# A four-layer graph-attention kernel: where the second step is prepared, a timetable for some steps, and the place of the copies of G

## The chip, the cores and the metric

The kernel runs on one core of one Trainium2 chip. Every time is device time in microseconds (us) for one execution of the program. Times of a run count from the first to the last instruction; the profile is one execution of the same program, recorded by the hardware profiler, and its times count from the start of its span.

TensorE (PE in the profile) multiplies matrices and writes to PSUM; PEld is its loading of the stationary operand. VectorE is DVE, ScalarE is ACT, GpSimd is POOL. SP is the engine whose queue issues nearly all transfers.

## What is computed

Sixteen samples `x[b]` of 1024 nodes by 256 features pass through four graph-attention layers over one 1024x1024 adjacency. Each layer is

```python
h = jnp.maximum(_layernorm(x), 0.0)
q = h @ W                                  # 256 features: 4 heads of 64, or 1 head of 256
e = leaky_relu(e_src[:, :, None] + e_dst[:, None, :])
attn = softmax(where(adj > 0, e, -inf))    # over the neighbours
x = x + elu(attn @ q)                      # relu in the last layer
```

Layers 0 and 2 have four heads, layers 1 and 3 have one. All arithmetic is float32.

## The kernel before

The work is cut into 64 **steps**, one for each pair of sample and layer. Four samples are in flight at a time (four streams), and `order_of_steps` writes the order of the 64 steps out: steps 0, 1 and 2 are layer 0 of samples 0, 1 and 2; step 3 is layer 1 of sample 0; then four-head and one-head steps alternate for most of the run. A stream comes back after three to five steps.

A step has three parts.

**Preparation** (`preparation(n)`) is a list of 21 pieces: statistics of the two halves of x on DVE (`stats`, L222), their combination on POOL (`combine_all`, L245 to L257), normalisation of the two halves on ACT (`normalise`, L263), and for each half two transposes (L271 on PE, L272 on ACT) and four projections (L282 on PE, L284 on ACT, followed by L290 and L292 on ACT and L294 on POOL). At the end `factors` (L300, L301) and `rows` (L306, L308) put a vector G for each head into a tile `gT`, and a transfer on the SP queue (L310) writes it to DRAM. `fetch_heads` then issues transfers (L324) that bring each head's G back, spread over all partitions, as `gs`.

**Aggregation**: for each head ACT copies `gs` into PSUM as `g` (`broadcast`, L330), DVE makes eight tiles `w` of 128x1024 from it (`weights`, L335), and PE multiplies them with the projected features (`aggregate`, L351). ACT takes the sums out of PSUM as `y` (L366). Each step has eight **groups** of aggregation: of a four-head step a group is half of the rows of one head, of a one-head step an eighth of the rows. There are two PSUM buffers for `g`, two for the sums, and 18 buffers for `w`, so DVE can be ahead of PE by 18 tiles.

**The end of a step** (`finish`): division, ELU and the addition to x, on DVE (L383, L392, L405), POOL (L393, L406) and ACT (L399).

The engines each work through their instructions in the order in which the program emits them, and this order is written by hand. The main loop goes through the groups; after each it emits pieces of the end of the step before, then those preparation pieces of later steps that are due, and then up to six (one-head: three) tiles `w`:

```python
emit_tiles(place[n, h, C - 1] + 1, must=True)
aggregate(n, h, i0, per)
...
prepare(8 * n + k)
ahead = 6 if per > 1 else 3
emit_tiles(min(done["tiles"] + ahead, done["free"] + WBUFS))
```

When a piece is due is said by an **agenda** of 21 numbers, in groups. For step n they are added to `8 * (n - 2)`, two steps ahead. `FOUR` serves four-head steps, `ONE` one-head steps, `SOON` the first ones, `FIRST` step 1 (its numbers are absolute). Where the stream isn't free at the first number of `FOUR`, `LATE` is taken instead, with a later start: before the change this falls on steps 7, 9 and 60, whose streams rested three steps in between (most four-head steps have rested four). A copy of G is emitted inside `emit_tiles`, when the tile four places ahead of the next tile belongs to a new head, and thus after the pieces of its group.

In the opening, before the main loop, step 0 is prepared at once, mixed with the building of the adjacency masks (`sign`, L178, L192, L195, L199). The transfers of x for samples 2 and 3 (`load`) and of the weights of layers 2 and 3 are issued at the end of the opening.

Of the kernel before, what the change touches and what calls it, by code (L numbers as in the profile page):

```python
# [38 lines left out]
WBUFS = 18  # L39
# [2 lines left out]

FOUR = (-8, -8, -5, -3, -2, -1, -1, 0, 0, 0, 0, 0, 0, 2, 2, 2, 2, 3, 8, 8, 10)
ONE = (2, 2, 2, 4, 4, 5, 5, 6, 6, 6, 6, 6, 6, 8, 8, 8, 8, 8, 10, 10, 12)
SOON = (0, 0, 0, 1, 2, 3, 3, 4, 4, 5, 5, 5, 5, 6, 6, 7, 7, 8, 9, 9, 11)
FIRST = (-2, -2, -2, -1, -1, 0, 0, 0, 0, 1, 1, 1, 1, 2, 2, 2, 2, 3, 3, 3, 5)
LATE = (0, 0, 0, 1, 1, 2, 2, 3, 3, 3, 3, 3, 3, 4, 4, 4, 4, 5, 6, 6, 8)


LAYERS = [
    (4, 0.2, 0, 0),
    (1, 0.2, 0, 0),
    (4, 0.2, 128, 1),
    (1, 0.01, 0, 1),
]
# [3 lines left out]
def kernel(ctx: ExitStack, tc: tile.TileContext, x, adj, ws, avs, out):  # L61
    nc = tc.nc
    B, N, F = x.shape
    C = N // P
# [46 lines left out]
    def load_weights(l, queue=nc.sync):  # L111
        H = LAYERS[l][0]
        for k in range(K):
            queue.dma_start(out=heads_of(wx[l], H)[:, k, :, 0:F // H],
                            in_=ws[l][k * P:(k + 1) * P, :].rearrange("p (h d) -> p h d", h=H))
# [87 lines left out]
    def load(b, parts=1):  # L203
        xs[b] = xpool.tile([P, C, F], F32, name="x")
        xb = x[b].rearrange("(p c) f -> p c f", p=P)
        for i in range(parts):
            q = slice(i * C // parts, (i + 1) * C // parts)
            nc.sync.dma_start(out=xs[b][:, q], in_=xb[:, q])
# [112 lines left out]
    def fetch(n, h):  # L321

        gs = state[n]["gs", h] = work.tile([P, N], F32, name="gs", bufs=2)
        nc.sync.dma_start(out=gs, in_=state[n]["grow"][h].rearrange("c i -> (c i)")  # L324
                          .partition_broadcast(P))

    def broadcast(n, h):

        g = state[n]["g", h] = ps_g.tile([P, N], F32, name="g")
        nc.scalar.activation(g, state[n]["gs", h], AF.Copy)  # L330

    def weights(n, h, jc):

        w = state[n]["w", h, jc] = work.tile([P, N], F32, name="w", bufs=WBUFS)
        nc.vector.scalar_tensor_tensor(w, state[n]["g", h], state[n]["rcol"][:, jc, h:h + 1],  # L335
                                       masks[LAYERS[steps[n][1]][3]][:, jc, :],
                                       op0=ALU.max, op1=ALU.mult)
# [88 lines left out]
    def groups(n):  # L426
        if LAYERS[steps[n][1]][0] == 1:
            return [(0, i, 1) for i in range(C)]
        return [(h, i, HALF) for h in range(LAYERS[steps[n][1]][0]) for i in (0, HALF)]

    tiles = [(n, h, jc) for n, (b, l) in enumerate(steps) for h in range(LAYERS[l][0])
             for jc in range(C)]
    place = {t: i for i, t in enumerate(tiles)}
    done = {"tiles": 0, "g": 0, "gs": 0, "rows": 0, "free": 0, "prepared": 0}
    agenda = []

    def prepare(upto):

        while agenda and agenda[0][0] <= upto:
            _, n, piece, last = agenda.pop(0)  # L440
            piece()
            if last:
                done["prepared"] = n + 1

    def plan(n):
        new = preparation(n)
        agenda.extend((at, n, piece, i == len(new) - 1) for i, (at, piece) in enumerate(new))
        agenda.sort(key=lambda a: a[:2])

    def fetch_heads(below=0):  # L450

        done["rows"] = max(done["rows"], below)
        while done["gs"] < min(done["g"] + 2 * C, len(tiles)):
            n, h, _ = tiles[done["gs"]]
            if n >= done["rows"]:
                break
            fetch(n, h)
            done["gs"] += C

    def emit_tiles(upto, must=False):  # L460
        while done["tiles"] < min(upto, len(tiles)):
            i = done["tiles"]

            while done["g"] <= min(i + C // 2, len(tiles) - 1):
                n, h, _ = tiles[done["g"]]
                if n >= done["prepared"]:
                    if i < done["g"] or not must:
                        break
                    prepare(max(a[0] for a in agenda if a[1] == n))
                broadcast(n, h)  # L470
                done["g"] += C
                fetch_heads()
            if i >= done["g"]:
                return
            weights(*tiles[i])
            done["tiles"] += 1

    last, agenda_of = {}, []
    for n, (b, l) in enumerate(steps):

        free = 8 * (last[b % STREAMS] + 1) + (8 if l == 0 else 2) if b % STREAMS in last else -99
        last[b % STREAMS] = n
        start = 8 * (n - 2)
        kind = ONE if LAYERS[l][0] == 1 else SOON if n < 4 else FOUR
        if free > start + kind[0]:
            kind = LATE
            start = max(free, agenda_of[-1][0] + 5, start - LATE[7])
        agenda_of.append([start + k for k in kind] if n > 1 else FIRST)
        if n > 2:

            assert agenda_of[n][7] >= 8 * (n - 2)
            was = agenda_of[n - 1]
            assert agenda_of[n][3] >= was[5] and agenda_of[n][4] >= was[11]
    ending = []
    later = {}
    with tc.manual_schedule():
        blocks = [mask_rows(c) for c in range(C)]
        layer = [weight_columns(l) for l in range(L)]
        layer[0][0](nc.scalar)
        load(0, 2)  # L500
        load_weights(0)
        for c in range(C):
            blocks[c][0]()
        load(1)
        load_weights(1)
        nc.scalar.activation(warm, half1, AF.Exp)
        nc.vector.tensor_copy(identb, ident)
        layer[0][1]()
        first = [piece for _, piece in preparation(0)]

        def sign(c):

            if c < C:
                blocks[c][1]()
                blocks[c][2]()
            if c > 0:
                blocks[c - 1][3]()

        for i in (0, 1, 3, 4):
            first[i]()  # L520
        layer[0][2]()
        first[5]()
        first[6]()
        layer[0][3]()
        sign(0)
        for i, c in ((7, 1), (9, 2), (11, 3), (13, 4), (15, 5)):
            first[i]()
            first[i + 1]()
            sign(c)
        for piece in first[17:]:  # L530
            piece()
        for c in (4, 5, 0, 1, 2, 3):
            blocks[c][4]()
        sign(6)
        sign(7)
        sign(8)
        done["prepared"] = 1
        plan(1)
        planned = 2
        for _ in range(2):  # L540
            agenda.pop(0)[2]()
        emit_tiles(C, must=True)
        blocks[6][4]()
        blocks[7][4]()
        prepare(-1)
        for i in range(2, STREAMS):
            load_weights(i)
            load(i)

        for l, at in ((1, 1), (2, 8 * 3 + 3), (3, 8 * 5 + 3)):  # L550
            for i, piece in zip((0, 1, 2, 8), layer[l]):
                later[at + i] = piece
        for n in range(len(steps)):
            for k, (h, i0, per) in enumerate(groups(n)):
                while planned < len(steps) and min(
                        a[0] for a in agenda_of[planned:planned + 2]) <= 8 * n + k:
                    plan(planned)
                    planned += 1
                emit_tiles(place[n, h, C - 1] + 1, must=True)
                aggregate(n, h, i0, per)  # L560
                if i0 + per == C:
                    done["free"] = place[n, h, C - 1] + 1
                while ending and ending[0][0] <= k:
                    ending.pop(0)[1]()
                if 8 * n + k in later:
                    later[8 * n + k]()
                prepare(8 * n + k)
                ahead = 6 if per > 1 else 3
                emit_tiles(min(done["tiles"] + ahead, done["free"] + WBUFS))
            for _, piece in ending:  # L570
                piece()
            ending = finish(n) if n < len(steps) - 1 else []
# [35 lines left out]
```

## Time and profile before

| | |
|---|---|
| time of three runs | 2640.95 to 2642.32 us, median 2642.26 |
| span of the profile | 2639.2 us |
| PE busy | 2539.8 us (96%) |
| DVE busy | 2041.7 us (77%) |
| ACT busy | 1133.4 us (43%) |
| POOL busy | 1021.5 us (39%) |
| mean granted clock of TensorE | 0.989 |

PE is the busiest engine by far. Its busy time leaves 99 us of the span, and a part of its work is also done at a lower clock. The profile's table of 40 slices of 66 us shows that most slices leave PE about 1 us idle; the first few, the seventh and the last four leave more.

### The profile page before, as it was taken

The page shows a single profiled execution, that of the slowest core. Times are in us where ns is not written, and L with a number is a line of the kernel's source. Part 1 is how long each engine was busy: PE and PEld are TensorE (multiplying, and loading weights), DVE is VectorE, ACT ScalarE, POOL GpSimd, SP SyncE. Part 2 cuts the span into 40 slices and gives each one's busy share as a digit, 9 for nine tenths or more (in the row PEclk, how much of TensorE's full clock was granted, in tenths as well). Part 3 has the DMA queues.
Part 4 walks back from the last instruction along what each step waited for, and adds up shares of the span by engine and source line. Part 5 has one row for each costly group of instructions (what it writes and reads, how often), then busy time and mean ns, then how long its engine had stood idle before and what let it go on. Part 6 is the DMA issues. An engine that isn't in the chain of part 4 may idle for free.

```text
span 2639.2 us, 87794 instructions
## 1 busy us (share of the span) xinstructions
PE 2539.8 (96%) x40088; PEld 2256.5 (86%) x40088; DVE 2041.7 (77%) x2144; ACT 1133.4 (43%) x2502; POOL 1021.5 (39%) x1040
## 2 busy tenths in 40 slices
PE   6899998999999999999999999999999999999899
PEld 4788887888888888888898888888888888888888
DVE  7888566877778877778877778877778877777973
ACT  4343443344444344544344444344444344443341
POOL 2234353423433434443323444433433334444231
PEclk8999999999999999999999999999999999999999
DMA  4101001111112100102211101101112200111101
GB/s 176 51 27 42 26 26 34 42 49 67 50 58 74 42 19 34 42 34 74 74 54 62 42 34 42 42 20 65 50 58 74 74 19 34 42 34 43 51 18 56
DMA packets 36987, 128.98 MB, mean 49 GB/s; under 512 B 6278, under 2 KB 9094, under 8 KB 34696
## 3 DMA queue, kind: packets, MB, share of 16 engines
q1 hardware_dynamic: 36606, 123.36, 13.3%
q8 instruction: 314, 5.14, 0.8%
q14 instruction: 57, 0.47, 0.1%
q10 hardware_dynamic: 10, 0.00, 0.0%
HBM read 105.91 MB, written 17.43 MB: 47 GB/s over the span
## 4 chain that ended last, share of the span: by engine, by line
PE 66%; DVE 17%; POOL 7%; ACT 6%; issue 3%; DMA 0%; DVEq 0%; ACTq 0%
PE acc L351 46%; PE pp L282 15%; DVE w L335 10%; PE pp L271 4%; POOL x L406 3%; DVE e L405 3%; DVE bn L222 2%; ACT xn L263 2%; POOL rstd L251 2%; ACT e L399 1%; DVE e L392 1%; ACT whx L284 1%; ACT rcol L290 0%; ACT gcol L301 0%; ACT whx L292 0%
## 5 line engine op out<-in xcount | busy, mean ns | idle before, releaser
L351 PE MATMUL acc<-whx,w 128*64 128x65 f32 x36864 | 1911.6, 241 | 26.0 <-DVE w L335 20.9
L351 PEld LDWEIGHTS acc<-whx,w 128*64 128x64 f32 x36864 | 1747.2, 145 | 171.6 <-issue 31.2
L335 DVE SCALAR_TENSOR_TENSOR w<-g,rcol,mask 128x1024 f32<-128x1024 f32 x1280 | 1540.6, 1273 | 445.5 <-PE acc L351 387.4
L366 ACT ACTIVATE y<-acc 128x260 f32<-128x260 f32 (+1 forms) x504 | 194.4, 386 | 1097.5 <-PE acc L351 1097.5
L294 POOL TENSOR_TENSOR whx<-whx 128x1024 f32<-128x1024 f32 x128 | 256.4, 2003 | 667.1 <-ACT whx L292 667.1
L282 PE MATMUL pp<-wx,hT 128*128 128x264 f32 (+1 forms) x2048 | 488.6, 390 | 18.8 <-ACT whx L284 11.2
L393 POOL TENSOR_TENSOR y<-y,r 128x1024 f32<-128x1024 f32 x126 | 264.3, 2108 | 618.7 <-DVE e L392 490.8
L282 PEld LDWEIGHTS pp<-wx,hT 128*128 128x128 f32 x2048 | 379.6, 191 | 98.7 <-ACT whx L284 23.5
L406 POOL TENSOR_TENSOR x<-x,e 128x1024 f32<-128x1024 f32 x96 | 238.1, 2486 | 161.0 <-DVE e L405 155.5
L263 ACT ACTIVATE xn<-x,shift,rstd 128x256 f32<-128x256 f32 x512 | 261.3, 590 | 87.9 <-POOL shift L257 85.8
L284 ACT ACTIVATE whx<-pp 128x264 f32<-128x264 f32 (+1 forms) x512 | 195.7, 386 | 236.4 <-PE pp L282 236.1
L222 DVE BATCH_NORM_STATS2 bn<-x 128x6 f32<-128x256 f32 x512 | 175.8, 410 | 58.0 <-POOL x L406 54.6
L405 DVE SCALAR_TENSOR_TENSOR e<-e,y 128x1024 f32<-128x1024 f32 x96 | 175.6, 1839 | 41.7 <-ACT e L399 35.5
L271 PE MATMUL pp<-ident,xn 128*128 128x128 f32 x1024 | 168.6, 284 | 32.1 <-ACT xn L263 28.4
L271 PEld LDWEIGHTS pp<-ident,xn 128*128 128x128 f32 x1024 | 119.3, 141 | 83.2 <-ACT xn L263 53.6
L330 ACT ACTIVATE g<-gs 128x1024 f32<-128x1024 f32 x160 | 163.6, 1024 | 8.1 <-DVE w L335 4.1
L272 ACT ACTIVATE hT<-pp 128x512 f32<-128x512 f32 x256 | 136.8, 585 | 1.9 <-PE pp L271 0.5
L251 POOL TENSOR_TENSOR rstd<-rstd,neghalf 128x8 f32<-128x8 f32 (+1 forms) x65 | 107.0, 1647 | 12.6 <-DVE shift L252 7.6
L399 ACT ACTIVATE e<-e 128x1024 f32<-128x1024 f32 x96 | 100.7, 1049 | 23.9 <-DVE e L392 20.0
L392 DVE SCALAR_TENSOR_TENSOR e<-y,r 128x1024 f32<-128x1024 f32 x64 | 75.5, 1221 | 2.2
L408 DVE SCALAR_TENSOR_TENSOR x<-y,x 128x1024 f32<-128x1024 f32 x30 | 43.3, 1444 | 10.0 <-POOL y L393 10.0
L245 POOL TENSOR_TENSOR dev<-bn 128x8 f32<-128x8 f32 x63 | 13.2, 209 | 89.8 <-DVE bn L222 89.8
(63 smaller groups left out, 401.7 us busy)
## 6 DMA issues: line engine op xcount, KB each, us to landing
gs<-grow SPq DMA_DIRECT2D x160, 512.0 KB
x<-in_x SPq DMA_DIRECT2D x15, 1024.0 KB
out<-x SPq DMA_DIRECT2D x30, 512.0 KB
w<-in_adj SPq DMA_DIRECT2D x8, 512.0 KB
x<-in_x SPq DMA_DIRECT2D x2, 512.0 KB
wx<-in_L_gnn_W SPq DMA_DIRECT2D x8, 128.0 KB
out<-x SPq DMA_DIRECT2D x8, 128.0 KB
grow<-gT SPq DMA_DIRECT2D x32, 16.0 KB
```

The source lines that it names most:

```text
L222: nc.vector.bn_stats(bn[:, c, :], xs[b][:, c, :])
L263: nc.scalar.activation(xn[:, q, :], xs[b][:, c, :], AF.Identity, bias=st["shift"][:, c:c + 1], scale=st["rstd"][:, c:c + 1])
L271: nc.tensor.transpose(pt[:, q, :], st["xn", half][:, q, k * P:(k + 1) * P], ident)
L282: nc.tensor.matmul(pw, lhsT=st["hT", half][:, k, q * P:(q + 1) * P], rhs=wx[l][:, k, :], start=(k == 0), stop=(k == K - 1))
L284: nc.scalar.activation(st["whx"][:, c, :], pw, AF.Copy)
L294: nc.gpsimd.tensor_tensor(wh[:, :, :, 0:D], wh[:, :, :, 0:D], wh[:, :, :, D:D + 1].to_broadcast([P, HALF, H, D]), op=ALU.mult)
L335: nc.vector.scalar_tensor_tensor(w, state[n]["g", h], state[n]["rcol"][:, jc, h:h + 1], masks[LAYERS[steps[n][1]][3]][:, jc, :], op0=ALU.m ...
L351: nc.tensor.matmul(acc[o % P:o % P + cols, q, :], lhsT=st["w", h, jc][:, o:o + cols], rhs=st["whx"][:, jc, h * (D + 1):(h + 1) * (D + 1)], ...
L366: nc.scalar.activation(st["y"][:, i0:i0 + per, h, :], acc, AF.Copy)
L393: nc.gpsimd.tensor_tensor(yh, yh, rb, op=ALU.mult)
L405: nc.vector.scalar_tensor_tensor(e, e, -1.0, yh, op0=ALU.add, op1=ALU.max)
L406: nc.gpsimd.tensor_add(xh, xh, e)
```

## The change

The change has four parts, all of them in the order of emission; no instruction is new and none is left out.

1. **Opening.** Step 1's statistics and their combination are emitted before the last three mask blocks, its normalisation right after the first eight tiles `w`, and everything else of its preparation, up to `rows`, before the main loop begins, so that PE has step 1's transposes and projections before step 0's first aggregation. They used to be spread over the groups of step 0. The new `FIRST` says this: nearly all its numbers are -1.
2. **Agendas.** A new agenda `SHORT`, `FOUR` with its first four pieces later (from -4 on, not from -8), is taken by four-head steps whose stream isn't free for `FOUR` in time: steps 7, 9 and 60. `LATE` isn't reached by them any more. Step 4 takes `SOON` and not `FOUR`.
3. **Copies of G.** A function `emit_heads` emits the copies that fall due in a group ahead of that group's preparation pieces, as far as the tiles of the head before last have all been emitted.
4. `emit_tiles` calls it too, and forces a step's preparation only where the next tile needs it.

```diff
+SHORT = (-4, -4, -4, -2, -2, -1, -1, 0, 0, 0, 0, 0, 0, 2, 2, 2, 2, 3, 8, 8, 10)
-FIRST = (-2, -2, -2, -1, -1, 0, 0, 0, 0, 1, 1, 1, 1, 2, 2, 2, 2, 3, 3, 3, 5)
+FIRST = (-2, -2, -2, -1, -1, -1, -1, -1, -1, -1, -1, -1, -1, -1, -1, -1, -1, -1, -1, -1, 3)
...
+    def emit_heads(i):
+        while done["g"] <= min(i + C // 2, done["tiles"] + C, len(tiles) - 1):
+            n, h, _ = tiles[done["g"]]
+            if n >= done["prepared"]:
+                break
+            broadcast(n, h)
+            done["g"] += C
+            fetch_heads()
+
     def emit_tiles(upto, must=False):
         while done["tiles"] < min(upto, len(tiles)):
             i = done["tiles"]
-            while done["g"] <= min(i + C // 2, len(tiles) - 1):
-                n, h, _ = tiles[done["g"]]
-                if n >= done["prepared"]:
-                    if i < done["g"] or not must:
-                        break
-                    prepare(max(a[0] for a in agenda if a[1] == n))
-                broadcast(n, h)
-                done["g"] += C
-                fetch_heads()
+            if i == done["g"] and tiles[i][0] >= done["prepared"] and must:
+                prepare(max(a[0] for a in agenda if a[1] == tiles[i][0]))
+            emit_heads(i)
...
-        kind = ONE if LAYERS[l][0] == 1 else SOON if n < 4 else FOUR
+        kind = ONE if LAYERS[l][0] == 1 else SOON if n < 5 else FOUR
+        if kind is FOUR and free > start + kind[0]:
+            kind = SHORT
         if free > start + kind[0]:
             kind = LATE
...
+        done["prepared"] = 1
+        plan(1)
+        planned = 2
+        prepare(-2)
         sign(6)
         sign(7)
         sign(8)
-        done["prepared"] = 1
-        plan(1)
-        planned = 2
+        emit_tiles(C, must=True)
         for _ in range(2):
             agenda.pop(0)[2]()
-        emit_tiles(C, must=True)
         blocks[6][4]()
         blocks[7][4]()
         prepare(-1)
         for i in range(2, STREAMS):
             load_weights(i)
             load(i)
...
+                upto = min(done["tiles"] + (6 if per > 1 else 3), done["free"] + WBUFS)
+                emit_heads(upto - 1)
                 if 8 * n + k in later:
                     later[8 * n + k]()
                 prepare(8 * n + k)
-                ahead = 6 if per > 1 else 3
-                emit_tiles(min(done["tiles"] + ahead, done["free"] + WBUFS))
+                emit_tiles(upto)
```

## The prediction, made before the changed kernel was run

> **What bounds the kernel now.** I read the page's slices first, then PE's waits by stretch, then the timelines of the stretches with waits.
>
> ```profile
> PE   6899998999999999999999999999999999999899
> PEclk8999999999999999999999999999999999999999
> ```
>
> Each digit is 66 us. From the ninth slice to the thirty-sixth PE has about 1 us idle a slice, in waits of 0.2 to 0.5 us; DVE waits there for PE (344.9 us in total between 470 and 2380 us, for buffers of w). So the middle is bound by PE's work, and a change of order gains next to nothing there. What can be won lies in the opening, in slices five to seven, and in the end. The opening on DVE and PE:
>
> ```profile
> 41.31 9.61 DVE L335 SCALAR_TENSOR_TENSOR w<-g,rcol,mask 128x1024 f32<-128x1024 f32 x8
> 50.84 2.70 DVE L222 BATCH_NORM_STATS2 bn<-x 128x6 f32<-128x256 f32 x8
> 53.46 19.14 DVE L335 SCALAR_TENSOR_TENSOR w<-g,rcol,mask 128x1024 f32<-128x1024 f32 x16
> 78.80 2.47 DVE L335 SCALAR_TENSOR_TENSOR w<-g,rcol,mask 128x1024 f32<-128x1024 f32 x2 [6.20 <-ACT g L330]
> ...
> 95.77 19.16 DVE L335 SCALAR_TENSOR_TENSOR w<-g,rcol,mask 128x1024 f32<-128x1024 f32 x16 [4.01 <-ACT g L330]
> ...
> 179.98 1.23 DVE L405 SCALAR_TENSOR_TENSOR e<-e,y 128x1024 f32<-128x1024 f32 x1 [9.35 <-ACT e L399]
> ```
>
> ```profile
> 42.73 0.48 PE L351 MATMUL acc<-whx,w 128*64 128x65 f32 x4 [5.21 <-DVE w L335]
> ...
> 185.92 22.57 PE L351 MATMUL acc<-whx,w 128*64 128x65 f32 x656
> 208.32 0.27 PE L306 MATMUL pp<-ident,gcol 128*32 128x128 f32 x1
> 208.43 1.90 PE L351 MATMUL acc<-whx,w 128*128 128x257 f32 x8
> ```
>
> PE has little to do from 31 to 51 us; then it is busy until DVE becomes the limit, from 96 to 165 us (DVE busy 68.93 of 69.00 us there, PE 58.70). DVE loses 6.20 and 4.01 us waiting for copies of G that stand behind preparation pieces on ACT. Step 3 starts on PE at 208.43. The transfers of the opening on SP's queue:
>
> ```profile
> 41.40 1.24 SPq L114 DMA_DIRECT2D wx<-in_L_gnn_W  x2
> 42.69 0.62 SPq L208 DMA_DIRECT2D x<-in_x  x1
> ```
>
> This is x of sample 2, which the statistics at 50.84 read without a wait. The later losses, on PE:
>
> ```profile
> 331.27 0.70 PE L351 MATMUL acc<-whx,w 128*128 128x257 f32 x2 [0.49 <-DVE w L335]
> ...
> 352.87 0.33 PE L271 MATMUL pp<-ident,xn 128*128 128x128 f32 x1 [1.89 <-ACT xn L263]
> ```
>
> ```profile
> 425.10 10.69 PE L351 MATMUL acc<-whx,w 128*128 128x257 f32 x48 [1.02 <-ACT y L366]
> 444.18 2.81 PE L271 MATMUL pp<-ident,xn 128*128 128x128 f32 x8 [8.38 <-ACT xn L263]
> 446.77 5.42 PE L351 MATMUL acc<-whx,w 128*128 128x257 f32 x16
> ```
>
> ```profile
> 414.85 7.24 DVE L335 SCALAR_TENSOR_TENSOR w<-g,rcol,mask 128x1024 f32<-128x1024 f32 x6 [1.38 <-ACT g L330]
> 422.01 0.34 DVE L383 RECIPROCAL r<-y 128x32 f32<-128x32 f32 x1
> ```
>
> ```profile
> 2406.30 0.33 PE L271 MATMUL pp<-ident,xn 128*128 128x128 f32 x1 [1.50 <-ACT xn L263]
> ```
>
> In each PE waits for a normalised x whose chain (end of the stream's last step, statistics, combination, normalisation) is late.
>
> **What the Trainium skill says.** "PSUM — Partial Sum Buffer", § Engine vs sequencer instructions, says that the queues of ScalarE, VectorE and GpSimd are strictly first in, first out; the trace agrees (the copy at 77.76 stood behind evacuations and normalisations on ACT while DVE waited 6.20 us). "TensorE: Matmul & The Clock Gate", Part 1, says that an idle PE falls to half its clock and comes back after a busy window of some 3.4 us. The trace agrees: granted clock 0.50 from 41 to 51 us, and after the 8.38 us wait eight transposes take 2.81 us instead of 1.10 to 1.30. "DMA: Bandwidth & Descriptors", on issuing engines not being separate queues, says that all transfers share the same 16 engines; what matters below is only the order on the issuing queue.
>
> **Part 1, the opening.** It moves 16 transposes (2.4 us) and 8 projections (3.83 us for four: 7.7), 10.1 us in all, from between the groups of step 0 into PE's gap. DVE's statistics of step 1 (2.70) go into its 3.34 us wait at 31 us, so the first tile comes when the copy of G is there, about 39.9 rather than 41.31.
> Then ACT: copies done at 40.9, normalisation 4.04, two masks 1.92, evacuation of two transposes 1.09: 48.0. PE: four projections 3.83, second half's transposes with evacuation 2.27 (92.54 to 94.81 in the old rows), four projections 3.83: 57.9; evacuation, exponentials, factors and rows some 2.5: 60.4. PE starts cold; half clock until 51 to 54.4 adds 1.5 to 3.1. So gT of step 1 is ready at about 62.5, and step 0's first group runs from there and not from 50.98.
> By itself this is about even: PE is later by 11.5 at the end of the first group and has 10.4 less to do. But the write of gT (L310) now stands on SP's queue **ahead** of the weights of layer 2 and of x of sample 2, and it waits for gT. So x of sample 2 is issued at 62.5 + 0.8 + 1.2 = 64.5, not at 42.69. Landing: at least 4.3 after issue (half of x was issued at 0.72 and awaited till 5.05), at most 8.2 (42.69 to 50.84); I take 6: 70.5. Behind it on DVE stand the statistics of step 2, emitted before tiles 8 to 13, and behind these all tiles: DVE, done with tile 7 at 49.4, idles for about 21 us. That is more than the 6.20 + 4.01 + 9.35 us of waits that the parts remove (the last two since copies and ends no longer stand behind so many pieces).
> From 70.5 DVE runs without a gap, since w buffers come free in time: statistics 2.7, then tiles 8 to 87, 80 x 1.195 (19.14/16) = 95.6, and between them columns of layer 1 3.3, two ends of steps 2 x (2.7 + 2.4), statistics of steps 3 and 4 2 x 2.7: 187.7. PE waits at that tile; then 3/4 of the group 2.9, three groups at 3.88, eight projections 7.7, transposes 1.2: step 3 starts at 211.1 instead of 208.43. Loss 2.7; with x two earlier or later and up to 3 for cold clock and copies that wait for DVE, -1 to +6. I take **3 slower**.
>
> **Part 2, agendas.** Step 9's `SHORT` takes its six tiles (7.24) and their copies out of DVE's way at 414 to 422: `rows` of step 9 falls in 8.0.0 and the tiles start in 8.0.2 (step, head, group), as in every later pair. So the division of step 7 comes at 413.9 instead of 422.01, and 3.65 us of tiles leave the path before its last addition: 11 us earlier in a chain that was 8.38 late. Wait 8.38 + 1.02, cold transposes 1.6, cold group 5.42 - 3.48 = 1.9: 12.9, of which the later pairs keep 0.8 (two 0.17 waits and slow transposes at 525.80). Gain **12**.
> Step 7's does the same at 331 to 355: the division of step 5, at 335.90, can come at about 331. The waits of 0.98, 1.89 and 0.48 and the cold group (5.19 - 3.48) go: 5.0, taken as **4.5**.
> Step 60: its statistics move one group (3.7 us) ahead, more than the 1.50 + 0.48 us of wait; with slow transposes **2.4**, of which the later end, where DVE is the limit, takes nothing (its first tile at 2430 follows PE).
> Step 4's move to `SOON` is in the sum of part 1.
>
> **Part 3, copies.** In the pairs of the middle the order on ACT changes once: the third head's copy stands before the evacuation of two transposes (1.02 us later). Behind these PE has a whole group (3.9) before it reads them, which hides it. ACT might wait in the copy for DVE; the old copies waited 4.1 us for DVE in all of the run, and in the middle the tile in question is done 10 us before (about 530 against 540.9). Zero.
>
> **Sum:** +3 - 12 - 4.5 - 2.4 = -15.9: 2642.3 - 15.9 = 2626.4.
>
> **Rivals.** (a) The opening gains: if x of sample 2 came at about 50 as before, PE (from 62.5: 24 groups 93, preparation of steps 2 to 4 30.3, small ones 3, and some 11 of waits for DVE) reaches step 3 at about 200: 8 gained, 2642.3 - 8 - 18.9 = 2615. Against it stands the queue's order; for it, the gap of 20 us on PE. (b) The idle DVE costs more, as the copies wait for DVE with evacuations behind them and PE is cold: opening 10 slower, 2633. (c) The 8.38 us wait only moves, since POOL's additions (5.57) and combination (4.2) remain: gain 4 of 12 with the rest as forecast, 2634; with (b) 2640, hardly a change. (d) Slower: the copies hold up ACT in the middle, 1 us for each of some 27 pairs on PE's path, +27 - 16: 2653. Against it: the 3.9 us of slack.
>
> **How the numbers follow.** Forecast (2620 to 2632) 0.57, (a) 0.12, (b) 0.13, (c) 0.12, (d) 0.06. Faster by over 0.2% (below 2637): forecast, (a), (b) and a third of (c), 0.86; within it 0.08, from (c) with (b); slower 0.06. The range leaves out the lower part of (a), the end of (c) and (d): 2616 to 2636.
>
> **What would show it.** Right: a DVE wait of about 20 us for the DMA of x before L222 at some 70 us; no DVE wait for g of 4 us or more before 200; step 3's first group (128x257) near 211; no wait over 1 us for xn between 340 and 460 nor at 2406; waits of the middle as before. Wrong: no such DVE gap (then (a)), a wait for xn still at about 440 (c), or ACT waiting tens of us for DVE in L330 copies (d).

## The result and the profile after

The changed kernel takes 2628.74 us in the median of four runs (2627.74 to 2632.07); the kernel before took 2641.61 us in four runs beside them (2639.95 to 2642.32). The ratio is 0.9954 with a 95% interval of 0.9937 to 0.9972: faster by some 12 to 13 us. The span of the profile falls from 2639.2 to 2626.9 us, by 12.3.

The sum of the forecast, 2626.4, is 2.3 us off, but its two main terms are off in opposite directions and partly make up for each other. The opening costs 8.4 us, not 3; the agendas bring 20.7 us, not 18.9. The opening can be separated from the rest, because PE has done exactly the same instructions in all kernels of this study when it comes to the four small matmuls that bound the scores of layer 3 (L154 before, L156 after), in step 6. I use this row as a checkpoint. It is the timeline of PE, of before and then of after; the columns are start, length, engine, line, operation, output and inputs, tile, elements and count.

```profile
343.42 0.50 PE L154 MATMUL pp<-sq,ones 128*128 128x1 f32 x4
```

```profile
351.80 0.50 PE L156 MATMUL pp<-sq,ones 128*128 128x1 f32 x4
```

After is 8.4 us later here. From here to the end of the span it needs 2626.9 - 351.8 = 2275.1 us, where before needed 2639.2 - 343.4 = 2295.8: 20.7 us less.

The slices of after, as they were shown for before:

```profile
PE   6889999999999999999999999999999999999899
PEclk8889999999999999999999999999999999999999
```

The second and third slice (66 to 198 us) have lost a tenth of the clock, and the third also one of PE. The seventh (396 to 462 us) shows no dip any more, where before had an 8. The loss lies in the opening, the gain where `SHORT` is taken; the experiments below try both. Now the rows behind them. The queue of SP in the opening, in after:

```profile
61.51 0.69 SPq L312 DMA_DIRECT2D grow<-gT  x1
62.25 2.14 SPq L116 DMA_DIRECT2D wx<-in_L_gnn_W  x2
64.43 0.61 SPq L210 DMA_DIRECT2D x<-in_x  x1
```

Before issued this x (sample 2) at 42.69. Now the write of `gT` stands ahead of it, and that write had to wait for the whole preparation of step 1. DVE in after, with the wait ahead of a row and its releaser in brackets:

```profile
40.16 9.63 DVE L337 SCALAR_TENSOR_TENSOR w<-g,rcol,mask 128x1024 f32<-128x1024 f32 x8 [0.95 <-ACT g L332]
69.43 2.71 DVE L224 BATCH_NORM_STATS2 bn<-x 128x6 f32<-128x256 f32 x8 [19.64 <-DMA x<-in_x]
72.05 21.53 DVE L337 SCALAR_TENSOR_TENSOR w<-g,rcol,mask 128x1024 f32<-128x1024 f32 x18
...
182.88 1.23 DVE L407 SCALAR_TENSOR_TENSOR e<-e,y 128x1024 f32<-128x1024 f32 x1 [4.02 <-ACT e L401]
```

The statistics of step 2 wait 19.64 us for that x, and 18 tiles stand behind them that needed nothing from it. The two waits for copies of G (6.20 and 4.01 in before) are gone, and the wait for the exponential has shrunk from 9.35 to 4.02. PE in after:

```profile
47.66 5.93 PE L284 MATMUL pp<-wx,hT 128*128 128x264 f32 x16 [2.93 <-ACT hT L274]
...
61.11 7.69 PE L353 MATMUL acc<-whx,w 128*64 128x65 f32 x256
73.47 0.49 PE L353 MATMUL acc<-whx,w 128*64 128x65 f32 x4 [4.68 <-DVE w L337]
...
173.01 3.81 PE L284 MATMUL pp<-wx,hT 128*128 128x258 f32 x8 [4.44 <-ACT whx L286]
...
214.98 7.11 PE L353 MATMUL acc<-whx,w 128*128 128x257 f32 x32
```

PE uses its old gap for the preparation of step 1 (from 42 to 61 us), runs two groups with the eight tiles that DVE had made before its wait and then, from 73, works at the pace of DVE's single tiles. Three stretches of after show it; the columns are the stretch, its length, the busy time of PE, PEld, DVE, ACT and POOL with the number of instructions, the granted clock, and the share and rate of DMA.

```profile
61.00:69.00 8.00, 7.79 (x257) 7.55 (x256) 0.00 (x0) 1.74 (x4) 1.25 (x1) 1.00 0.55 172
73.00:82.00 9.00, 3.68 (x34) 2.38 (x35) 9.00 (x9) 2.08 (x4) 2.92 (x7) 0.50 0.06 24
82.00:166.00 84.00, 79.12 (x1965) 73.25 (x1965) 83.80 (x84) 32.44 (x66) 20.68 (x21) 0.93 0.13 47
```

DVE does nothing at all from 61 to 69 us while PE is busy; then DVE is busy 9.00 of 9.00 us while PE, at half clock, works 3.68; and up to 166 DVE stays full (83.80 of 84.00). What DVE lost before 69 us can't be made up in that time.

The later places are those of the forecast. PE in after, where before waited 8.38 us at 444.18:

```profile
437.33 0.66 PE L273 MATMUL pp<-ident,xn 128*128 128x128 f32 x2
438.15 0.33 PE L273 MATMUL pp<-ident,xn 128*128 128x128 f32 x1 [0.16 <-ACT xn L265]
438.64 0.76 PE L273 MATMUL pp<-ident,xn 128*128 128x128 f32 x5 [0.16 <-ACT xn L265]
439.24 3.64 PE L353 MATMUL acc<-whx,w 128*128 128x257 f32 x16
```

PE where before waited 1.89 us at 352.87, and where it waited 1.50 us at 2406.30:

```profile
359.20 1.03 PE L273 MATMUL pp<-ident,xn 128*128 128x128 f32 x8
360.07 3.64 PE L353 MATMUL acc<-whx,w 128*128 128x257 f32 x16
...
2394.80 1.41 PE L273 MATMUL pp<-ident,xn 128*128 128x128 f32 x8
2396.05 3.64 PE L353 MATMUL acc<-whx,w 128*128 128x257 f32 x16
```

In all three places the wait is gone (two of 0.16 us are left in the first), and the group behind the transposes takes 3.64 us; after the long wait it took 5.42.

### The profile page after: what moved, and what is told of

It is laid out like the page before. It is cut to its first block, busy times and chain, and to the rows that moved or that the text cites. A ratio compares the mean times of both kernels' runs of the same rounds, so it can differ in the third digit from the quotient of the medians.

```text
span 2626.9 us, 87790 instructions
## 1 busy us (share of the span) xinstructions
PE 2536.5 (97%) x40088; PEld 2254.3 (86%) x40088; DVE 2046.0 (78%) x2144; ACT 1128.9 (43%) x2502; POOL 1020.9 (39%) x1040
## 4 chain that ended last, share of the span: by engine, by line
PE 64%; DVE 18%; POOL 7%; ACT 6%; issue 4%; DMA 1%; SPq 0%; DVEq 0%; ACTq 0%
PE acc L353 44%; PE pp L284 15%; DVE w L337 11%; PE pp L273 4%; POOL x L408 4%; DVE e L407 3%; DVE bn L224 2%; ACT xn L265 2%; POOL rstd L253 2%; ACT e L401 1%; DVE e L394 1%; ACT whx L286 1%; ACT rcol L292 0%; DMA x<-in_x 0%; ACT whx L294 0%
## 5 line engine op out<-in xcount | busy, mean ns | idle before, releaser
L353 PE MATMUL acc<-whx,w 128*64 128x65 f32 x36864 | 1905.3, 241 | 23.0 <-DVE w L337 20.7
```

Source lines behind the costliest of these rows:

```text
L353: nc.tensor.matmul(acc[o % P:o % P + cols, q, :], lhsT=st["w", h, jc][:, o:o + cols], rhs=st["whx"][:, jc, h * (D + 1):(h + 1) * (D + 1)], ...
```

## The experiments

Two questions were open after the result. First, why does the opening cost what it costs: because x of sample 2 stands behind the write of `gT` on one queue, or because the new opening itself is worse (a cold PE, and copies and evacuations in each other's way)? Second, do the agendas bring the later gain alone? All kernels were timed beside the kernel before, and the ratios are to it. Four experiments (x first, the opening of before, the opening alone, the agendas alone) shared runs of before with a median of 2642.45 us, the other four shared runs with a median of 2643.32; beside the changed kernel it was 2641.61. So a difference between kernels of different sets is certain only to some 2 us.

**The load of x ahead of the write.** The loads at the end of the opening (x of samples 2 and 3, and weights) are issued ahead of the rest of step 1's preparation; nothing else is changed in the changed kernel.

```diff
-        prepare(-1)
         for i in range(2, STREAMS):
             load_weights(i)
             load(i)
+        prepare(-1)
```

> The changed kernel with one edit: the transfers of the weights of layers 2 and 3 and of x of samples 2 and 3 are issued before step 1's rows and not behind them. Theory Q (queue): the opening costs about 10 us (step 3's first group at 214.98 instead of 204.74) because x of sample 2 stands on SP's queue behind the write of step 1's gT. Then DVE's wait of 19.64 us for the transfer of x goes, DVE waits later and shorter for w buffers, and step 3 starts at 200 to 205: 2628.7 - 12 = 2617 (2613 to 2620). Rival F (front-loading): it costs because PE makes all of step 1's preparation, partly at half clock, before its first aggregation. Then DVE's wait turns into one for w buffers and step 3 still starts near 215: 2627 to 2630.

2615.38 us (2615.06 to 2615.83), ratio 0.9895 (0.988 to 0.991); 13.4 us less than the changed kernel, whose interval doesn't touch this one. DVE in this kernel:

```profile
49.99 2.71 DVE L224 BATCH_NORM_STATS2 bn<-x 128x6 f32<-128x256 f32 x8 [0.32 <-DMA x<-in_x]
52.62 9.61 DVE L337 SCALAR_TENSOR_TENSOR w<-g,rcol,mask 128x1024 f32<-128x1024 f32 x8
66.41 12.01 DVE L337 SCALAR_TENSOR_TENSOR w<-g,rcol,mask 128x1024 f32<-128x1024 f32 x10 [4.18 <-ACT g L332]
```

The wait for x is 0.32 us instead of 19.64. PE still reaches the first aggregation only at 61.07, but now finds tiles for three groups in a row. The second row is where step 3 starts:

```profile
61.07 11.42 PE L353 MATMUL acc<-whx,w 128*64 128x65 f32 x384
...
199.01 7.11 PE L353 MATMUL acc<-whx,w 128*128 128x257 f32 x32
```

Step 3 starts at 199.01, 16 us before the changed kernel's 214.98 and 5.7 before the old kernel's. The queue's order is the cause of the loss; the new opening as such gains.

**The late x left late, tiles in front of the statistics.** If the queue only hurts because of what stands behind the statistics on DVE, then it is enough to put tiles ahead of them. Step 2 gets an agenda of its own; x of sample 2 is issued as late as in the changed kernel.

```diff
+        if n == 2:
+            kind = (2, 2, 2, 2, 2) + SOON[5:]
```

> The changed kernel (x of sample 2 still behind the write of step 1's gT) with one edit: step 2's statistics and normalisation stand two groups later, behind tiles 8 to 19. Theory: the late x costs only because DVE's statistics wait for it in front of these tiles; then DVE makes tiles 8 to 17 while x is on its way, its wait for x is under 5 us and step 3 starts at 200 to 204: 2628.7 - 12 = 2617. Rival: the late x costs by itself, since step 2's preparation comes late for PE: 2624 or more.

2616.51 us (2615.05 to 2617.5), ratio 0.9898 (0.9883 to 0.9914). DVE in this kernel:

```profile
39.82 19.16 DVE L337 SCALAR_TENSOR_TENSOR w<-g,rcol,mask 128x1024 f32<-128x1024 f32 x16 [1.28 <-ACT g L332]
65.58 4.86 DVE L337 SCALAR_TENSOR_TENSOR w<-g,rcol,mask 128x1024 f32<-128x1024 f32 x4 [6.60 <-ACT g L332]
70.35 2.70 DVE L224 BATCH_NORM_STATS2 bn<-x 128x6 f32<-128x256 f32 x8
```

Twenty tiles are done before the statistics at 70.35, which then find x there. Nearly the whole of the loss is gone with the transfer as late as ever (issued at 63.85). So the transfer's time was no loss in itself: the in-order queue of DVE turned it into one.

The 6.60 us are a wait for the copy of step 0's third G. That G doesn't depend on step 1's `gT`; the copy stands on ACT behind the evacuation of the first group, which waits for PE:

```profile
64.23 0.39 ACT L368 ACTIVATE y<-acc 128x260 f32<-128x260 f32 x1 [3.63 <-PE acc L353]
64.52 1.02 ACT L332 ACTIVATE g<-gs 128x1024 f32<-128x1024 f32 x1
```

PE starts that group late because it makes step 1's preparation first. This is a cost of the new opening itself; the first experiment has it too, with 4.18 us.

**The changed kernel with the opening of before.** `FIRST` and the order of the opening go back; agendas and copies stay.

```diff
-FIRST = (-2, -2, -2, -1, -1, -1, -1, -1, -1, -1, -1, -1, -1, -1, -1, -1, -1, -1, -1, -1, 3)
+FIRST = (-2, -2, -2, -1, -1, 0, 0, 0, 0, 1, 1, 1, 1, 2, 2, 2, 2, 3, 3, 3, 5)
...
-        prepare(-2)
         sign(6)
         sign(7)
         sign(8)
...
-        emit_tiles(C, must=True)
         for _ in range(2):
             agenda.pop(0)[2]()
+        emit_tiles(C, must=True)
```

> The changed kernel with the opening and the agenda of step 1 as before (parts 2 and 3 alone). If parts 2 and 3 bring what the two traces say between step 3 and the end (22.5 us) and are without effect on the opening: 2641.6 - 22.5 = 2619. If the copies ahead of the pieces also take away the 6.20 and 4.01 us for which DVE waited for g, and DVE is the limit behind them, up to 8 less: 2611. If those gains needed the new opening: above 2625.

2623.43 us (2620.95 to 2627.14), ratio 0.9926 (0.9911 to 0.9941). It passes the checkpoint at 343.72, where the kernel before is at 343.42. So the changed kernel would be some 5.3 us faster without its first part: no run of either kernel reaches into the range of the other, though the intervals of the two ratios just touch. In the profiles this is 8.1 us at the checkpoint, of which 2.7 are lost again in the rest; no single row was found for these.

**The new opening alone, on the kernel before.** The same edit the other way round.

> The kernel before with the new opening and the new agenda of step 1 only (part 1 alone). Theory: the part by itself costs what step 3's start shows, 10 us: 2641.6 + 10 = 2652, and more, up to 2656, since copies of G still stand behind pieces on ACT. Rival: the cost comes from the parts together (copies that wait for DVE ahead of evacuations); then this is within 4 us of 2642.

2652.48 us (2650.19 to 2654.66), ratio 1.0037 (1.0023 to 1.0051): 10 us slower than before, and measurably so. The wait for x is there (20.05 us), the checkpoint comes at 351.59, 8.2 us late. The waits of the old agendas stay; PE in this kernel:

```profile
361.05 0.33 PE L271 MATMUL pp<-ident,xn 128*128 128x128 f32 x1 [1.90 <-ACT xn L263]
...
451.93 2.80 PE L271 MATMUL pp<-ident,xn 128*128 128x128 f32 x8 [8.41 <-ACT xn L263]
```

Both are as long as in before (1.89 and 8.38), though PE comes to them 8 us later. So these waits don't depend on how late the kernel runs; the chain behind them moves along with it.

**The agendas alone, on the kernel before.**

```diff
+SHORT = (-4, -4, -4, -2, -2, -1, -1, 0, 0, 0, 0, 0, 0, 2, 2, 2, 2, 3, 8, 8, 10)
...
-        kind = ONE if LAYERS[l][0] == 1 else SOON if n < 4 else FOUR
+        kind = ONE if LAYERS[l][0] == 1 else SOON if n < 5 else FOUR
+        if kind is FOUR and free > start + kind[0]:
+            kind = SHORT
```

> The kernel before with SHORT for steps 7, 9 and 60 and SOON for step 4, copies and opening as before (part 2 alone). Theory: the waits for xn at 352, 444 and 2406 go by the agendas alone, so 2641.6 - 5 - 12.5 - 2.4 = 2622 (2619 to 2625). Rival: the copies ahead of the pieces are needed for the second; then the wait near 444 keeps 4 us or more, and the time is 2628 or more.

2622.31 us (2620.83 to 2624.64), ratio 0.9922 (0.9907 to 0.9936): 20.1 us less than before, more than the whole change. The wait for `xn` near 440 is two waits of 0.16, while the waits for copies of G in the opening (6.67 and 4.01) stay. The gain lies behind the checkpoint, in the places of `SHORT`, and it comes without the other parts.

**The copies alone, on the kernel before**, that is `emit_heads` and its calls.

> The kernel before with the copies of G ahead of a group's pieces and nothing else (part 3 alone). Theory from the runs so far (agendas alone -20.1 us, agendas and copies -19.0): the copies bring nothing by themselves, 2642 within 4 us. Rival: they take the 6.20 and 4.01 us for which DVE waited for g out of the opening, and PE gains most of it: 2634 or less.

2645.26 us in 20 runs (2641.47 to 2649.32), ratio 1.001 (1.0003 to 1.0017): slower by 0.1%, nearly nothing. The first of the two waits for copies of G goes, but the second grows; DVE in this kernel:

```profile
96.34 14.39 DVE L337 SCALAR_TENSOR_TENSOR w<-g,rcol,mask 128x1024 f32<-128x1024 f32 x12 [9.72 <-ACT g L332]
```

9.72 us stand in the place of 6.20 + 4.01. A wait taken from DVE at one tile came back at a later one.

**The mended opening without the new copies.** The first experiment with the copies of G as they were before, inside `emit_tiles` and behind a group's pieces.

> The kernel with x of sample 2 ahead of step 1's rows, but the copies of G emitted as before, behind a group's pieces (parts 1 and 2 with the queue mended, no part 3). Theory: copies don't matter: 2615.4 within 3 us. Rival: with a mended opening DVE waits for g behind the pieces of steps 2 to 4, 5 us or more: 2620 or more.

2615.85 us (2615.61 to 2616.18), ratio 0.9897 (0.9879 to 0.9914), against 2615.38 and 0.9895 with the new copies. In the time they make no difference that can be measured here either. The profiles say a little more: step 3 starts at 201.42 with the old copies and at 199.01 with the new ones, and 1.6 of these 2.4 us are given back by a stretch of half clock that the kernel with the new copies happens to have (last section). So a gain of some 2 us from the copies in the mended opening is not excluded.

**The exponential later.** In the changed kernel PE waits 4.44 us for evacuations of projections at 173 us, and 3.73 us for others near the end of the run; in the first experiment both waits are 4.44 us. ACT in the changed kernel says why:

```profile
166.67 0.39 ACT L368 ACTIVATE y<-acc 128x260 f32<-128x260 f32 x1 [2.43 <-PE acc L353]
171.63 1.06 ACT L401 ACTIVATE e<-e 128x1024 f32<-128x1024 f32 x1 [4.56 <-DVE e L394]
172.59 0.64 ACT L286 ACTIVATE whx<-pp 128x258 f32<-128x258 f32 x2
```

The exponential of step 1's end stands in ACT's queue ahead of the evacuation of projections that PE has already made, and it waits 4.56 us for a product of DVE, which has its own tiles to do first. So PE waits for the evacuation. The experiment moves this exponential one group later, on top of the first experiment, where a four-head step is followed by another one (steps 0, 1 and 59).

```diff
         at = (0, 0, 0, 0, 1, 1, 1) if H > 1 else (0, 0, 1, 1, 2, 2, 3)
+        if H > 1 and LAYERS[steps[n + 1][1]][0] > 1:
+            at = (0, 0, 0, 1, 1, 1, 1)
```

> The kernel with x of sample 2 ahead of step 1's rows, and in addition the first exponential of a step's end emitted one group later where a four-head step follows a four-head step (after steps 0, 1 and 59). Theory: PE's wait of 4.44 us for the evacuation of projections in step 2's first group, and the one of 3.73 us in step 60's, arise because the exponential, which waits for DVE, stands ahead of these evacuations on ACT; both go, and with the clock that they cost: 2615.4 - 8 = 2607 (2605 to 2610). Rival: PE is only waiting for DVE in another place, and runs into waits for w instead: 2613 to 2616.

2609.2 us (2607.74 to 2610.99), ratio 0.9871 (0.9856 to 0.9887): 6.2 us less than the first experiment, and the fastest kernel of the study, 19.5 us below the changed one. PE in this kernel:

```profile
151.24 3.75 PE L284 MATMUL pp<-wx,hT 128*128 128x258 f32 x16
...
169.56 0.33 PE L273 MATMUL pp<-ident,xn 128*128 128x128 f32 x1 [2.87 <-ACT xn L265]
```

The 4.44 us are gone, and sixteen projections run in one piece, but 2.87 us for a normalised x come up behind. Step 3 starts at 197.86, only 1.15 us before that of the first experiment. At the checkpoint it is 2.7 us ahead (334.70 against 337.41), but 1.6 of these are the clock of one stretch again (last section). In the rest it gains 4.0 (2271.9 against 2275.9); the 4.44 us wait near the end is gone there.

The parts side by side, all from the profiles:

| kernel | checkpoint, us | from there to the end, us |
|---|---|---|
| before | 343.42 | 2295.8 |
| opening alone | 351.59 | 2296.8 |
| copies alone | 344.08 | 2298.2 |
| agendas alone | 345.77 | 2275.4 |
| agendas and copies (opening of before) | 343.72 | 2277.8 |
| the change | 351.80 | 2275.1 |
| the change, x ahead of the write | 337.41 | 2275.9 |
| the same, old copies | 338.25 | 2275.6 |
| the change, tiles ahead of the statistics | 339.18 | 2275.9 |
| x ahead of the write, exponential later | 334.70 | 2271.9 |

The right column has two levels, some 2296 to 2298 without `SHORT` and 2275 to 2278 with it (and 2271.9 with the later exponential). The left column depends mostly on the opening.

## Why the forecast held, and which term was mis-sized

**The queue and the wait behind it: right.** The write of `gT` was forecast for 62.5 and issued at 61.51, x of sample 2 for 64.5 and issued at 64.43; its statistics were forecast for 70.5 and ran at 69.43, after 19.64 us of idle DVE where about 21 were forecast. The first two experiments, which remove either side of this, bring 13.4 and 12.2 us against the changed kernel. Rival (a), worked out for an x that came in time, gave step 3 at about 200 and 2615 us; the first experiment has 199.01 and 2615.4.

**The opening as a term: 3 us forecast, 8.4 measured at the checkpoint.** Three pieces make up the difference.

- The start from which the loss was counted was misread. The forecast took 208.43 for step 3's first group. In the timeline of before one row can hold instructions of several shapes and is named after the first; the row at 185.92 with 656 instructions holds five groups of 128 and 16 more. A window that begins at 204.9, after the last row of the four-head step, shows these, and that step 3 started at 204.74:

```profile
204.74 3.74 PE L351 MATMUL acc<-whx,w 128*128 128x257 f32 x16
208.32 0.27 PE L306 MATMUL pp<-ident,gcol 128*32 128x128 f32 x1
```

 That is 3.7 us: even with the forecast's own 211.1, the loss would have been 6.4.
- Step 3 of after starts at 214.98, 3.9 us after the forecast's 211.1; PE has the same instructions behind it there as before had at 204.74. DVE was counted without a gap from 70.5 on, with each end of a step at its own duration. In fact ACT, PE and DVE held each other up once at the end of step 1: ACT 4.56 us for DVE, PE 4.44 us for ACT, DVE 4.02 us for ACT. All three stand in the rows above. The forecast had no such wait; the old kernel's 9.35 us wait for the same exponential was taken as removed, and 4.02 of it was left. The sum bears this out: the tile that PE was to wait for, the sixth in DVE's row of 22 that begins at 184.02, was done at some 191.2 and not at 187.7, though DVE had started a little earlier than forecast; from there PE needed 23.8 us, where 23.4 were forecast. No experiment shows it by itself: moving the exponential in the last experiment brought only 1.15 us before step 3, and a wait for `xn` came up there.
- Against this, 1.6 us came back. A hundred matmuls of the 128x65 form, at 272.13 in before, took 4.71 us; the same hundred, at 282.26 in after, took 3.14. The 10.2 us of step 3's start (214.98 - 204.74) are 8.6 in the row after these. No part of the change explains this (last section).

So 2.7 + 3.7 + 3.9 - 1.6 = 8.7, of which 8.4 are measured at the checkpoint. The rival with an opening 10 us slower was closer for this term.

**The agendas: 18.9 forecast, 20.7 measured.** The delay of after against before, read at the starts of equal rows of PE, falls in steps:

| row of PE | before, us | after, us | after - before | gained since the row above |
|---|---|---|---|---|
| checkpoint | 343.42 | 351.80 | 8.4 | |
| projections of step 8 | 360.10 | 363.55 | 3.4 | 4.9 (step 7, forecast 4.5) |
| projections of step 10 | 452.03 | 442.72 | -9.3 | 12.8 (step 9, forecast 12) |
| projections of step 59, ahead of step 60's wait | 2370.66 | 2360.73 | -9.9 | 0.6 (the middle, forecast 0) |
| the group behind step 60's transposes | 2408.37 | 2396.05 | -12.3 | 2.4 (step 60, forecast 2.4) |

The chain that the forecast walked through for step 9 is the one that moved. The division of step 7 was to come 8.1 us earlier (at 413.9 instead of 422.01). DVE in after:

```profile
417.32 0.34 DVE L385 RECIPROCAL r<-y 128x32 f32<-128x32 f32 x1
```

It runs at 417.32 while PE is 3.4 us behind the kernel before, so 8.1 us earlier for its place. The wait went with nothing in its place, and rival (c), that the wait only moves, is out.

**The copies: nothing forecast, nothing found.** Alone they cost 0.1%, with the rest they make 0.5 us. ACT's copies waited 8.3 us for DVE in the whole run, 4.1 before; rival (d) needed tens. From 460 to 1250 us PE's waits for `xn` sum to 5.1 us, 5.2 before; from 1250 to 2370 to 6.5 us, 6.1 before.

So the term of the forecast that was mis-sized is the opening: the start of step 3 in before was misread, and DVE was counted as running without a gap. That the sum came within 2.3 us is in part luck: 5.4 us too little loss in the opening stand against 1.8 too little gain in the agendas, which leaves 3.6, and 1.3 of these went with the starting point, since the forecast counted from the median of 2642.3 and the profiled run of before, from which the terms are measured, took 2640.99.

**What stays open.** The parts alone sum to -20.1 + 10.0 + 1.9 = -8.2 us, and together they make -12.9. In the profiles a part of this lies ahead of the checkpoint (8.2 + 2.4 + 0.7 = 11.2 for the parts, 8.4 together) and a part behind it (1.0 - 20.4 + 2.4 = -17.0 for the parts, -20.7 together). The hundred matmuls don't explain it: their 1.6 us are gained in the opening alone, in the copies alone and in the change. The cause was not tried. The agendas alone pass the checkpoint 2.4 us later than before, although PE has done the same work there. `SOON` prepares step 4 later than `FOUR` did: its statistics run at 165.82 us, in before at 117.50. At 166.2 the two kernels have PE rows of the same work at nearly the same time, but the agendas alone have eight transposes of step 4 still to do and have waited 4.44 us and not 3.27 for an evacuation; step 3 then starts at 207.36, in before at 204.74. So the later preparation of step 4 is the likely cause, but it was not tried by itself.

## What to carry to other kernels

When work is moved to an earlier place, follow every queue that its instructions stand on, that of the transfers first: an issue that waits holds up the issues behind it, and the cost shows on another engine, at whatever stands behind the first reader of the late data. Put work that is ready (here tiles) ahead of work that waits for a transfer, and a late transfer can cost little: on DVE this won back 12.2 of 13.4 us here. And test the parts of a change one at a time: here one part alone brought 20 us and another alone cost 10, which a ratio of 0.995 for the whole doesn't show.

## What the runs showed of the hardware that was not expected

The same hundred matmuls of the 128x65 form, after three small waits (0.48, 0.85 and 0.86 us in after, 0.47, 0.85 and 0.86 in before), have one of two durations. PE's timeline in before, and then in after:

```profile
272.13 4.71 PE L351 MATMUL acc<-whx,w 128*64 128x65 f32 x100 [0.86 <-DVE w L335]
```

```profile
282.26 3.14 PE L353 MATMUL acc<-whx,w 128*64 128x65 f32 x100 [0.86 <-DVE w L337]
```

The kernel with x ahead of the write, the one with tiles ahead of the statistics and the agendas alone have the 4.71 of before; all other kernels have the 3.14 of after. The wait just ahead is 0.85 or 0.86 us in all ten. The difference is the granted clock. Here is a part of this stretch in before, and the whole of it in after (columns as above):

```profile
272.88:276.29 3.41, 3.41 (x70) 3.41 (x68) 3.41 (x4) 0.00 (x0) 0.00 (x0) 0.50 0.02 5
```

```profile
282.26:285.40 3.14, 3.14 (x101) 3.07 (x101) 3.14 (x9) 0.00 (x0) 0.41 (x2) 1.00 0.02 5
```

The four kernels with 4.71 were all granted half the clock for 3.41 or 3.42 us in this stretch, the six with 3.14 the full clock throughout. So waits of under 1 us were followed by half clock in some of these kernels and not in others. The Trainium skill, "TensorE: Matmul & The Clock Gate", Part 1, says that the window over which PE's activity is judged runs freely and doesn't start with the kernel; the two levels agree with that, though no run here shows where the window lies. There is one profile of each kernel, so it is not shown whether the same kernel changes its level from one execution to the next. In practice, 1.6 us between two orders of this kernel at such a place are no sign that one order is better.
